# Strassen products for w of layer 1 and for both wide products of layer 2, and layer 1's weights normalised ahead of its product

## The chip, the cores and the metric

One core of one Trainium2 chip. The metric is the device time of one execution in microseconds (us). Times are medians of the fast executions on one chip; one execution of all fell in the slow state, and it is named and left out. "TensorE records" are the records of matmuls in the trace: each f32 matmul leaves two (before, the 16 matmuls of layer 2's product for v leave 32, from 1280.02 us on).

## The reference, cut to what matters

128 graphs of 64 nodes with 512 features each, and an adjacency (64 x 64) for each graph, pass through four graph layers. Each layer works on h = relu(layer norm of x) and is added to x.

```python
h = maximum(_layernorm(x), 0); x = x + _L0(h, adj, ...)   # layer 0: 512 -> 1024 -> 512
# layer 1
y = x @ w;  s = y @ a                                     # x here is h
A = exp(leaky(tanh((s_i + s_j) / 8) * 8)) * A_shape
A = A / sum(A, -1) * sum(A_shape, -1)
out = A @ x @ w                                           # w is 512 x 512
# layer 2
query, keyt, value = x @ Wq.T + bq, x @ Wk.T + bk, x @ Wv.T + bv
weight = adj * exp(query @ keyt.T)
out = (weight / sum(weight, 2)) @ value
# layer 3: three products of 512 x 512 with Wk[0..2] on x, T x, T T x
```

The inputs make b2, the bias of layer 0's second product, zero.

## The kernel before

Everything is f32. Sixteen groups of 512 rows (four tiles of 128) go through layers 0 and 1 first ("first half"), x is written to memory, and then all groups go through layers 2 and 3 ("second half"). The "change of half", some 1200 to 1400 us into the run, is where the last groups of the first half and the first groups of the second are worked on together.

Layers 0 and 3 already use Strassen's method in Winograd's form: a product of 2 x 2 blocks takes seven block products instead of eight, with sums of blocks before (in the code `comb`) and additions of the products after it (`U`, `emit`). Layer 1's product with w and layer 2's products for q (Wq and Wk folded into one matrix, `wg`) and v are plain:

```python
    def layer1(g):
        ...                                   # scores: dots with w a, tanh, leaky, exp
        for s in HALVES:
            dve(0.42, lambda s=s: nc.vector.tensor_mul(PT.t[s, :, s], z.t[s], ad.t[s, 1]), ...)
        dve(0.42, lambda: nc.vector.tensor_reduce(rows.t, ad.t[:, 0], AX.X, ALU.add), [ad], [rows])
        pd = col_sums(PT, PTk)                # four one-column matmuls
        ...                                   # sc = rows / pd, 128 x 4
        for t in range(T):
            ph = left_mul_T(hs[t], lambda t=t: PT.t[:, t, :], PTk, "mT")
            proj(lambda c, ph=ph: ph.t[:, c, :], lambda c: w_sb[:, c, :], p, ...)   # 4 matmuls of 512 columns
            dve(0.75, ... xx = p * sc + xx)   # the scale is put on the output
    def layer2(g):
        ...
        for o in range(KD):                   # q: 4 x 4 matmuls of 512 columns
            proj(lambda c, oc=oc: wg_sb[:, c, oc], lambda c: hT.t[:, c, :], pq, ...)
            ...
        for t in range(T):                    # v: 4 x 4 matmuls of 512 columns
            proj(lambda c, t=t: hT.t[:, c, tok(t)], lambda c: wv_sb[:, c, :], p, ...)
```

The program orders its own instructions while it is built. Every operation states its engine, a cost in us and a precedence number (`G.prio`, lower goes first). A list scheduler repeatedly takes, for each engine, the operation that can start earliest, and uses the precedence only among those that could start at the same time:

```python
                    if t0 is None or (t, o.prio, o.seq) < (t0, pick.prio, pick.seq):
                        t0, pick = t, o
    ...
    STRETCH, PERIOD1, PERIOD2 = 2.5, 80.0, 60.0
    for g in range(NG):
        ...
        G.prio = g * PERIOD1
        layer0(g); layer1(g)
    load_w("wg", ...); load_w("wv", ...)      # over w1's place
    olds2 = [keys of w2 and its sums, keys of w]
    ... loads of Wk3 (layer 3's weights) over olds2 ...
    W3 = combine("w3", ...)                   # four block sums of the weights on VectorE
    for g in range(NG):
        G.prio = NG * PERIOD1 + g * PERIOD2
        layer2(g); layer3(g)
```

Each engine gets its queue in that order.

Of the kernel before, what the change touches and what calls it, by code (L numbers as in the profile page):

```python
# [13 lines left out]
P = 128  # L14
C = 64
# [139 lines left out]
def tile_adj_preln_d4(  # L155
# [17 lines left out]
        "x": ([P, D], 8), "adj": ([P, 2, T, C], 3), "h": ([P, D], 5), "o": ([P, D], 2),  # L173
        "u5": ([P, 3, D], 1), "u2": ([P, 3, D // 2], 2), 
# [3 lines left out]
    }  # L178
    TWO = [
        (("tmp", [P, D], 4), ("s3", [P, 3, 6, P], 1)),  # L180
        (("z", [P, DH], 2), ("hT", [P, KD, T * P], 1)),
        (("rT", [P, KH, P], 3), ("a3", [P, 3 * KD, P], 2)),
        (("s2", [P, 3, 4, P], 1), ("vu", [P, D], 3)),
        (("y", [P, D], 2), ("qT", [P, T * P], 2)),
        (("mT", [P, KD, P], 3), ("a3", [P, 3 * KD, P], 1)),
        (("s1", [P, 3, 2, P], 2), ("tt", [P, T, 2, P], 1)),
# [4 lines left out]
    for old, new in TWO:  # L191
        size = lambda shape: shape[1] * (shape[2] if len(shape) > 2 else 1) * (shape[3] if len(shape) > 3 else 1)
        both = work.tile([P, max(size(old[1]) * old[2], size(new[1]) * new[2])], F32, name=f"{old[0]}_{new[0]}")
        for tag, shape, n in (old, new):
            for i in range(n):
                v = both[:, i * size(shape):(i + 1) * size(shape)]
                if len(shape) == 3:
                    v = v.rearrange("p (a b) -> p a b", a=shape[1])
                elif len(shape) == 4:
                    v = v.rearrange("p (a b c) -> p a b c", a=shape[1], b=shape[2])  # L200
                slots.setdefault(tag, []).append(v)
        after.setdefault(new[0], []).append(old[0])
# [12 lines left out]
    w_sb = view(WB, 7168, KD, D)  # L215
    wg_sb = view(WA, 0, KD, D)
    wv_sb = view(WA, 2048, KD, D)
# [9 lines left out]
    def c_v(n, from_psum=False):  # L227
        return n / 960 + (0.22 if from_psum else 0.16)
# [32 lines left out]
    sel = const.tile([2, 2, P], F32, name="sel")  # L261
    for i in range(2):
        nc.vector.tensor_copy(sel[:, i, :], ident[0:2, i:i + 1].to_broadcast([2, P]))
# [4 lines left out]
    def load_w(name, sb, src, olds=()):  # L268
        k, n = src.shape[0] // P, src.shape[1]
        v = src.rearrange("(c p) o -> p c o", p=P)  # L270
        for c in range(0, k, 2):
            dma(2 * n / 2, lambda c=c: nc.sync.dma_start(sb[:, c:c + 2, :], v[:, c:c + 2, :]), [], [(name, c // 2), *olds])
# [4 lines left out]
    def load_row(name, src):  # L277
        sb = const.tile([P, src.shape[0]], F32, name=name)
        dma(P * src.shape[0] * 4 / 1024, lambda: nc.sync.dma_start(sb, src.partition_broadcast(P)), [], [name])
        return sb  # L280
# [37 lines left out]
    b1_b = load_row("b1_b", b1)  # L318
# [4 lines left out]
    b2_b = load_row("b2_b", b2)  # L323
# [5 lines left out]
    wa_b = const.tile([P, D], F32, name="wa_b")  # L329
# [3 lines left out]
    bw2_b = const.tile([P, D], F32, name="bw2_b")  # L333
# [26 lines left out]

    def setup_l0():


        p, row = Buf("ps"), Buf("o")
# [10 lines left out]
        pe(c_mm(512, 1), lambda: nc.tensor.matmul(pm.t, sel[:, 0, :], row.t[0:2, :], start=True, stop=True), [row], [pm])  # L375
        pe(c_mm(512, 1), lambda: nc.tensor.matmul(pb.t, sel[:, 1, :], row.t[0:2, :], start=True, stop=True), [row], [pb])
        act(0.6, lambda: nc.scalar.copy(bw2_b, pb.t), [pb], ["bw2"])
# [5 lines left out]
    def spread(col, dst, r, key):  # L383
# [5 lines left out]
        act(0.6, lambda: nc.scalar.copy(dst, p.t), [p], [key])  # L389

    def setup_l1():
        wa, a_b = Buf("col"), temp(a.partition_broadcast(P))
        for c in range(KD):
            dot(lambda c=c: w_sb[:, c, :], lambda: a_b.t, lambda c=c: wa.t[:, c:c + 1], [("w", c // 2), a_b], [(wa, c)])
        spread(lambda: wa.t, wa_b, [(wa, c) for c in range(KD)], "wa")
# [22 lines left out]
    def setup_l3():  # L418
# [3 lines left out]
        for s in range(2):  # L422
# [5 lines left out]
            spread(lambda cc=cc: cc.t, c3_b[:, s, :], [(cc, c) for c in range(KD)], ("c3", s))  # L428
# [44 lines left out]

    def strassen(A, keys, B, kc, n, stag, emit):

# [11 lines left out]
        def prod(p, lhs, kl, b, first):  # L487
            rhs, kb = B[b]

            def mm():  # L490
                for c in range(kc):
                    nc.tensor.matmul(p.t[:, :n], lhs()[:, c, :], rhs(c), start=first and c == 0, stop=c == kc - 1,  # L492
                                     skip_group_check=True)
            pe(c_mm(n, kc), mm, [*kl, *kb] if first else [*kl, *kb, p], [p])
            step(c_mm(n, kc))

        p1, p2, p3, p4 = (Buf("ps") for _ in range(4))
        c1, u2, u3 = ((U, i) for i in range(3))
        prod(p1, a[0, 0], keys[0, 0], "11", True)
# [4 lines left out]
        act(n / 1200 + 0.17, lambda: nc.scalar.copy(U.t[:, 0], p1.t[:, :n]), [p1], [c1])  # L504
        prod(p2, s2, [(S, 1)], "T2", True)
        dve(c_v(n, True), lambda: nc.vector.tensor_add(U.t[:, 1], p2.t[:, :n], U.t[:, 0]), [p2, c1], [u2])  # L506
# [386 lines left out]
```

## Time and profile before

| | before |
|---|---|
| time, median of 3 | 2655.7 us (2651.23 to 2656.02) |
| profiled execution, span | 2648.8 us, clock 1.0 |
| TensorE busy, records | 2628.4 us, 10970 |
| VectorE busy | 1503.4 us |
| GpSimd busy | 520.6 us |

The kernel's fast executions spread from 2650.6 to 2656.2 us, on every chip about as wide (28 executions on four chips). The ratios below carry that as part of their interval.

The prediction shows the page and TensorE's waits. The busy times of the engines in a stretch stand in one line: TensorE, TensorE's weight loads, VectorE, ScalarE, GpSimd with the number of instructions behind each, then TensorE's clock, the DMA share and GB/s.

```profile
1200.00:1500.00 300.00, 297.18 (x1213) 200.00 (x1212) 154.70 (x376) 83.81 (x141) 37.26 (x55) 1.00 0.13 46
```

TensorE's order in time is shown by start, duration, source line, output and inputs, shape, number of records, and in brackets an idle time with what ended it.

```profile
1302.35 1.88 PE L636 MATMUL ps<-y_qT,bd 128*128 128x512 f32 x4
1304.07 3.60 PE L471 MATMUL ps<-wa_mem,z_hT 128*128 128x512 f32 x8
1307.50 3.94 PE L696 MATMUL ps<-y_qT,z_hT 128*128 128x128 f32 x32
1311.28 0.60 PE L541 MATMUL ps<-dg,ones_bd 128*128 128x256 f32 x2
1313.17 1.05 PE L562 MATMUL ps<-ones,bd 128*128 128x1 f32 x8 [1.29 <-DVE bd L703]
```

L636 is layer 0's last product, L541 the score product of layer 1's last group. Between the two lies a serial chain: x, its statistics, h, the dots with w a (the vector w times a, which the scores need). During its 7 to 9 us TensorE works at layer 2's first group, a plain product for q (L471, 3.4 us) and its scores (L696, 3.8 us), and L541 comes without a wait. Only layer 2's own column sums (L562) wait 1.3 us. So plain products of layer 2 hide layer 1's last chain.

### The profile page before, as it was taken

What the parts mean: (1) busy time and instruction counts of PE and PEld (TensorE: products, weight loads), DVE (VectorE), ACT (ScalarE), POOL (GpSimd) and SP (SyncE); (2) the same over time, 40 slices, a digit from 0 to 9 for tenths busy, and PEclk for the clock granted to TensorE, in tenths of its full rate; (3) what the DMA queues carried; (4) which work ended last, traced back from release to release, by engine and by line L of the source; (5) the groups of instructions that cost most, each with busy time, mean ns of one, the idle gap of its engine ahead of it and who ended that gap; (6) DMA issues with size and microseconds to landing.
All of it is one profiled execution on the core that took longest, in us unless ns stands there. A gap on an engine that the chain in (4) does not pass through costs nothing.

```text
span 2648.8 us, 28910 instructions
## 1 busy us (share of the span) xinstructions
PE 2628.4 (99%) x10970; PEld 1826.4 (69%) x10970; DVE 1503.4 (57%) x3618; ACT 787.4 (30%) x1338; POOL 520.6 (20%) x651
## 2 busy tenths in 40 slices
PE   8999999999999999999999999999999999999999
PEld 5666666666666666666567767777677766777677
DVE  8777676667666666766445443454435444354434
ACT  3343333334233333333222222222222222222221
POOL 4222223323222332222101111110111111111101
PEclk9999999999999999999999999999999999999999
DMA  4021100011100001111021000100011001100000
GB/s 159 33 92 36 36 24 17 32 37 36 36 29 22 27 32 37 36 36 44 28 84 36 29 28 33 36 20 28 25 36 36 20 21 32 36 32 16 21 24 25
DMA packets 53196, 95.99 MB, mean 36 GB/s; under 512 B 7744, under 2 KB 7744, under 8 KB 53056
## 3 DMA queue, kind: packets, MB, share of 16 engines
q1 hardware_dynamic: 53056, 94.14, 10.5%
q8 instruction: 86, 1.41, 0.2%
q14 instruction: 54, 0.44, 0.0%
HBM read 59.52 MB, written 34.60 MB: 36 GB/s over the span
## 4 chain that ended last, share of the span: by engine, by line
PE 99%; DVE 1%; ACT 0%; issue 0%; DMA 0%; DVEq 0%; ACTq 0%
PE ps L492 51%; PE ps L471 25%; PE ps L460 4%; PE ps L770 4%; PE ps L696 2%; PE ps L716 2%; PE ps L624 2%; PE ps L636 2%; PE ps L681 1%; PE ps L761 1%; PE ps L562 1%; PE ps L751 1%; PE ps L584 1%; PE ps L404 1%; PE ps L541 1%; PE ps L371 0%
## 5 line engine op out<-in xcount | busy, mean ns | idle before, releaser
L443 POOL TENSOR_TENSOR rs<-ve,mhalf 128x1 f32<-128x1 f32 x320 | 213.9, 671 | 1408.5 <-DVE ve L442 1376.3
L492 PE MATMUL ps<-wb_mem,rT_a 128*128 128x256 f32 x2056 | 472.7, 379 | 1.0 <-ACT u L504 1.0
L492 PEld LDWEIGHTS ps<-wb_mem,rT_a 128*128 128x128 f32 x2056 | 386.0, 190 | 61.9 <-issue 6.2
L451 ACT ACTIVATE h<-x,nm,rs 128x512 f32<-128x512 f32 x256 | 205.4, 811 | 356.5 <-DVE nm L450 353.7
L492 PE MATMUL ps<-wb_mem,tmp_s 128*128 128x256 f32 x1152 | 263.8, 379 | 0.0
L492 PEld LDWEIGHTS ps<-wb_mem,tmp_s 128*128 128x128 f32 x1152 | 215.6, 190 | 34.0 <-issue 4.1
L440 DVE BATCH_NORM_STATS2 st<-x 128x6 f32<-128x512 f32 x256 | 175.5, 686 | 110.5 <-DMA x<-xm 109.8
L492 PE MATMUL ps<-wa_mem,mT_a 128*128 128x512 f32 x512 | 237.9, 593 | 0.0
L471 PE MATMUL ps<-wa_mem,z_hT 128*128 128x512 f32 x512 | 228.2, 592 | 0.2 <-ACT z_hT L683 0.2
L471 PE MATMUL ps<-wb_mem,mT_a 128*128 128x512 f32 x512 | 227.4, 592 | 0.0
L471 PE MATMUL ps<-z_hT,wa_mem 128*128 128x512 f32 x512 | 227.3, 592 | 0.0
L492 PE MATMUL ps<-wb_mem,s_vu 128*128 128x256 f32 x768 | 180.1, 380 | 0.0
L492 PE MATMUL ps<-wa_mem,s_tt 128*128 128x512 f32 x384 | 177.7, 593 | 0.4 <-DVE s_tt L485 0.4
L471 PEld LDWEIGHTS ps<-wb_mem,mT_a 128*128 128x128 f32 x512 | 96.1, 190 | 114.8 <-issue 114.3
L471 PEld LDWEIGHTS ps<-z_hT,wa_mem 128*128 128x128 f32 x512 | 95.0, 190 | 101.7 <-issue 100.9
L471 PEld LDWEIGHTS ps<-wa_mem,z_hT 128*128 128x128 f32 x512 | 94.8, 190 | 100.4 <-issue 99.0
L492 PEld LDWEIGHTS ps<-wa_mem,mT_a 128*128 128x128 f32 x512 | 93.7, 190 | 100.0 <-issue 100.0
L492 PEld LDWEIGHTS ps<-wb_mem,s_vu 128*128 128x128 f32 x768 | 143.5, 190 | 21.4 <-issue 2.4
L460 PEld LDWEIGHTS ps<-bd,h 128*128 128x128 f32 x1024 | 129.3, 194 | 40.0 <-issue 34.7
L462 ACT COPY mT_a<-ps 128x512 f32<-128x512 f32 x128 | 74.6, 583 | 246.8 <-PE ps L460 206.6
L532 POOL TENSOR_TENSOR u<-u,bk_b 128x256 f32<-128x256 f32 x96 | 71.2, 757 | 365.0 <-DVE u L506 189.9
L460 PE MATMUL ps<-bd,h 128*128 128x128 f32 x1024 | 133.0, 278 | 4.3 <-ACT h L451 4.1
(163 smaller groups left out, 3525.1 us busy)
## 6 DMA issues: line engine op xcount, KB each, us to landing
x<-in_x_dram SPq DMA_DIRECT2D x64, 256.0 KB, 2.6
xm<-x SPq DMA_DIRECT2D x64, 256.0 KB, 2.0
x<-xm SPq DMA_DIRECT2D x64, 256.0 KB, 2.6
out_dram<-x SPq DMA_DIRECT2D x64, 256.0 KB, 2.0
adj<-in_adj_dram SPq DMA_DIRECT2D x32, 256.0 KB, 2.5
wb_mem<-in_Wk_dram SPq DMA_DIRECT2D x6, 512.0 KB, 7.2
wa_mem<-in_W1T_dram SPq DMA_DIRECT2D x2, 1024.0 KB, 8.1
wb_mem<-in_W2T_dram SPq DMA_DIRECT2D x4, 512.0 KB, 6.2
```

The costliest lines, as they stand in the source:

```text
L440: dve(0.69, lambda i=i: nc.vector.bn_stats(st.t[:, i, :], src(i)), [r[i]], [(st, i)])
L443: pool(0.57, lambda: nc.gpsimd.tensor_tensor(rs.t, ve.t, mhalf, ALU.pow), [ve], [rs])
L451: act(0.82, lambda: nc.scalar.activation(h.t, xx.t, AF.Relu, bias=nm.t, scale=rs.t), [xx, nm, rs], [h])
L460: nc.tensor.matmul(quad(p)[:, c, :], h.t[:, c * P:(c + 1) * P], rhs(), start=True, stop=True)
L462: act(0.59, lambda: nc.scalar.copy(m.t, quad(p)), [p], [m])
L471: nc.tensor.matmul(p.t, lhsT(c), rhs(c), start=first and c == 0, stop=last and c == k - 1)
L492: nc.tensor.matmul(p.t[:, :n], lhs()[:, c, :], rhs(c), start=first and c == 0, stop=c == kc - 1, skip_group_check=True)
L532: pool(0.75, lambda: nc.gpsimd.tensor_add(U.t[:, iv], U.t[:, iu], row[:, cols]), [u, krow], [v])
L624: nc.tensor.transpose(quad(pt)[:, c, :], z.t[:, j * D + c * P:j * D + (c + 1) * P], ident)
L636: pe(c_mm(512, 1), lambda y=y, pf=pf, t=t: nc.tensor.matmul(pf.t, M.t[:, t, :], y.t, start=True, stop=True), [(y, 0), (y, 1), *Mr], [pf])
L696: nc.tensor.matmul(quad(pl)[:, t, :], hT.t[:, o, tok(t)], qT.t[:, tok(t)], start=(o == 0 and t == 0), stop=(o == KD - 1), skip_group_check ...
L770: nc.tensor.matmul(pq.t[:, c * 2 * P:(c + 1) * 2 * P], h.t[:, cc * P:(cc + 1) * P], tt.t[:, t].rearrange("p j k -> p (j k)"), start=True, ...
```

## The change

The intent: 7/8 of the matmul work in three more products. TensorE is the bound (99% busy before), VectorE (57%) and GpSimd (20%) have time left for the extra sums. In layer 1 the scale of the output goes into the weights first, so that the additions after the Strassen products need no scale. In layer 2 the four block sums of h are shared by q and v (`sh`). The diff, cut to its core:

```diff
-        PT, rows, sc = Buf("bd"), Buf("col"), Buf("col")
+        PT, pd, rn = Buf("bd"), Buf("ps"), Buf("ee")
+        dve(0.42, lambda: nc.vector.tensor_mul(z.t, z.t, ad.t[:, 1]), [z, ad], [z])
+        def sums():
+            for i, m in enumerate((lambda: z.t, lambda: ad.t[:, 1])):
+                nc.tensor.matmul(pd.t[:, i * T * C:(i + 1) * T * C], ones_bd, m()..., start=True, stop=True)
+        pe(c_mm(256, 2), sums, [z, ad], [pd])
+        dve(2.0, lambda: nc.vector.reciprocal(rn.t, half(0)), [pd], [rn])
+        dve(0.42, lambda: nc.vector.tensor_mul(rn.t, rn.t, half(1)), [pd, rn], [rn])
         for s in HALVES:
-            dve(0.42, lambda s=s: nc.vector.tensor_mul(PT.t[s, :, s], z.t[s], ad.t[s, 1]), [z, ad], ...)
+            dve(0.42, lambda s=s: nc.vector.tensor_mul(PT.t[s, :, s], z.t[s], rn.t[s]), [z, rn], ...)
-        for t in range(T): ... proj(..., w_sb, ...)
+        for t0 in (0, 2):
+            ph = [left_mul_T(hs[t], ...) for t in (t0, t0 + 1)]
+            strassen(lambda i, j, ph=ph: ph[i].t[:, 2 * j:2 * j + 2, :], ..., W, 2, D // 2, "s1", emit_w)
@@ layer2
+        X = Buf("sh")                          # four sums of blocks of h, for q and v
+        for q, (a, ka, b, kb, op) in enumerate(...):
+            dve(c_v(D), lambda ...: nc.vector.tensor_tensor(X.t[:, q], a(), b(), op), ...)
-        for o in range(KD): ... proj(lambda c, oc=oc: wg_sb[:, c, oc], ...)
+        seven({n: prod(WG[n], hs[n], True) for n in range(1, 8)}, Buf("u5"), D, emit_q)
-        for t in range(T): ... proj(..., lambda c: wv_sb[:, c, :], ...)
+        seven({n: prod(WV[n], hv[n], False) for n in range(1, 8)}, Buf("u5"), D, emit_v)
@@ memory: which buffers of the second half (right) lie over which of the first (left)
-        (("s2", [P, 3, 4, P], 1), ("vu", [P, D], 3)),
-        (("s1", [P, 3, 2, P], 2), ("tt", [P, T, 2, P], 1)),
+        ([("s2", [P, 3, 4, P], 1), ("s1", [P, 3, 2, P], 2)], [("vu", [P, 2, D], 2), ("tt", [P, T, 2, P], 1)]),
+        ([("row", [P, D], 5)], [("sh", [P, 4, 2, 2 * P], 1)]),
-    wa_b = const.tile([P, D], F32, name="wa_b")
+    wa_b = Buf("row")                          # the row w a, which layer 1's dots read
@@ order and loads
-    STRETCH, PERIOD1, PERIOD2 = 2.5, 80.0, 60.0
+    STRETCH, PERIOD1, PERIOD2 = 2.5, 80.0, 65.0
+    W = combine("w", w_sb, w_x, 2, D // 2, "DVE")
+    WG, WV = combine_hT("wg", wg_sb, wg_x, True), combine_hT("wv", wv_sb, wv_x, False)
-    olds2 = [keys of w2 and its sums, keys of w]
+    olds2 = [keys of w2 and its sums, keys of w and its sums]
```

## The prediction

> **What bounds the kernel now.** I read the page first (busy shares, then the 40 slices), then the waits of TensorE, the stretches in which each engine was busy, and the order of TensorE's instructions in time.
>
> ```profile
> span 2648.8 us, 28910 instructions
> PE 2628.4 (99%) x10970; PEld 1826.4 (69%) x10970; DVE 1503.4 (57%) x3618; ACT 787.4 (30%) x1338; POOL 520.6 (20%) x651
> PEclk9999999999999999999999999999999999999999
> PE ps L584 <- DVE mB L579: 5.9, 1, 5.9
> PE ps L460 <- ACT h L451: 4.1, 2, 3.7
> PE ps L770 <- ACT s_tt L753: 1.4, 2, 0.7
> 300.00:1100.00 800.00, 800.00 (x3279) 530.62 (x3278) 545.86 (x1325) 284.82 (x488) 223.50 (x263) 1.00 0.09 32
> 1480.00:2480.00 1000.00, 1000.00 (x4267) 729.03 (x4266) 452.63 (x1114) 245.96 (x414) 121.74 (x168) 1.00 0.09 29
> ```
>
> TensorE is busy 99% of the span at an ungated clock (the windows give 1.00). Its longest wait is 5.9 us, once, at the very start; the nine waits in the whole list sum to about 16 us. In the two long windows (layers 0 and 1; then layers 2 and 3) it never stops, while VectorE has 32% and 55% left. So the time is the sum of TensorE's instructions plus a small fixed rest. What must be found is what one instruction costs in the stream. The duration in the group rows (379 ns for 256 columns, 592 for 512) is not that: consecutive matmuls overlap. I take start-to-start distances:
>
> ```profile
> 602.70 1.89 PE L492 MATMUL ps<-wb_mem,rT_a 128*128 128x256 f32 x8
> 604.42 1.89 PE L492 MATMUL ps<-wb_mem,s_vu 128*128 128x256 f32 x8
> 606.15 1.02 PE L636 MATMUL ps<-y_qT,bd 128*128 128x512 f32 x2
> 607.01 0.59 PE L541 MATMUL ps<-dg,ones_bd 128*128 128x256 f32 x2
> ...
> 685.25 0.59 PE L541 MATMUL ps<-dg,ones_bd 128*128 128x256 f32 x2
> ...
> 1280.02 13.90 PE L471 MATMUL ps<-z_hT,wa_mem 128*128 128x512 f32 x32
> 1293.76 3.60 PE L471 MATMUL ps<-wa_mem,z_hT 128*128 128x512 f32 x8
> ```
>
> Each f32 matmul leaves two records. 32 records of 512 columns take 1293.76-1280.02 = 13.74 us, 0.4294 each; 16 of 256 columns take 606.15-602.70 = 3.45 us, 0.2156 each. So a matmul costs 0.859 us at 512 columns and 0.431 at 256: cost goes with columns, halving the columns costs nothing extra, and a Strassen product of narrower matmuls is not punished. The same line of one group recurs after 685.25-607.01 = 78.24 us: one group's period in the first half. In the second half the row-sum line recurs after 83.8 us (1730.93 to 1814.73). Sixteen groups each: 16 x (78.24+83.8) = 2592.6; setup matmuls, start, change of half and tail make the rest of the 2648.8.
>
> [...] of the four block sums of 128x256 in layer 0, one kind takes 635 ns and another 415 (one line, L485)[...].
> [...] the reciprocal[...]. No run here yet shows a wide one; the narrow one (128x4) takes 178 ns against 162 for a product of that size.
>
> **The change, part by part.**
> *Layer 1, product with w.* Per group before: 4 tiles x 4 matmuls of 512 columns = 16 x 0.859 = 13.74 us. After: 2 pairs of tiles x 7 products x 2 matmuls of 256 columns = 28 x 0.431 = 12.07. Saved 1.67. The column sums (4 one-column matmuls, 8 records in 0.80 us) become two 256-column matmuls, 0.86: net saved 1.6 us.
> *Layer 2, q and v products.* Before: 2 x 16 x 0.859 = 27.49 us. After: 2 x 7 products x 4 matmuls of 256 columns = 56 x 0.431 = 24.14. Saved 3.3 us. The order of the changed program confirms the counts: 512-column matmuls fall from 1373 to 605, those of 256 rise from 2528 to 3904; other sizes change only by those 64 one-column ones.
> *Sum on TensorE.* -768 x 0.859 + 1376 x 0.431 - 12.8 = -659.7+593.1-12.8 = -79 us[...]. I use 78: new periods 76.7 and 80.5 us.
> *VectorE, layer 1, per group.* Added: 8 block sums of 128x256 at about 0.50 (mean of the four L485 kinds), 4 additions to U and 8 final ones at 0.42, one product of 128x256 at 0.42, a second at 0.42, and a reciprocal of 128x256.[...] Removed: 4 x 0.75, a row reduction 0.41, two small ones 0.34. Net about +8.4 us.
> *VectorE, layer 2, per group.* Added: 4 shared sums and 4+7 additions of 128x512 at 0.69 = 10.35; removed 4 x 0.69: +7.6. Total 16 x 16 = 256 us: busy goes from 1503 to about 1760 us, 68%. In the first half it is 545.9/800 x 78.24 = 53.4 per period, and 62 of 76.7 after (80%); in the second 37.9, and 45.5 of 80.5 (57%). Beside TensorE, therefore, not ahead of it.
> *GpSimd.* +6 additions of 128x256 (0.75) in layer 1, +6 of 128x512 (1.3) in layer 2: +12 us per group, 520 to about 715 us, 28%. ScalarE: about the same.
> *Setup.* Four more weight sums for w (1.2 us each, as the other 128x1024 ones), ten of 128x512 for layer 2: some 13 us of VectorE, at the start and at the change of half, with other work open. Both loads of layer 2 weights are there before and after.
>
> **What could eat the 78 us.** The sum holds only if TensorE still never waits. I walked the narrowest places of the new order by hand. In layer 2 the last transposes of h are followed by one layer 3 product (12 records, 2.59 us), then by the product that needs two shared sums. Copy out of PSUM begins about 0.2 after the transposes and takes 0.59, two sums take 1.35, hand-overs 0.2: 2.3 us of 2.59. For the first score matmuls of a combined q: after the seventh product U is added (0.2+0.65), GpSimd adds the bias (1.3), VectorE adds q (0.69), with 0.2 of hand-overs 3.0 us; two products lie between, 3.45 us. Both fit, with 0.3 to 0.5 us to spare.[...]
>
> **Rivals.**
> *A: Narrow chains and the GpSimd lock bring waits in every group.* For: slack of a third of a us, two engines more loaded[...], one slot each for U and for the shared sums. Against: the scheduling gave TensorE an unbroken 1800 us in the two windows, and costs stated in the code equal the trace (0.42, 0.69, 1.3). At 1 us per group in both halves 16-32 us return: 2594 to 2610.
> *B: VectorE becomes the bound in the first half.* For: 80% there, in order[...]. Against: 20% is left, and work of neighbouring groups is mixed. A third of the gain lost would mean about 2604.
> *C: The change of half gets longer,* because block sums now stand between loads and first products. For: about 5 us of small waits lie there today (1265, 1311, 1347 us). Against: raw blocks come first in the new order, combined ones some 12 us of TensorE work later. Worth 0 to 6 us: 2578 to 2584.
> *D: No gain, as narrower matmuls cost more each.* The spacings above refute it; it would give about 2655.
>
> **Range and chances.** 2655.7-78.0 = 2577.7. I add 3 us for small waits (C and a little of A): 2581. If start and change of half go better: 2568; if A takes a us per group all over: 2605. Two per cent lies at 2602.6, which needs 25 us of new waits. Chances: 0.89 faster, 0.10 within, 0.01 slower.
>
> **What would show it right or wrong.** Right: TensorE has 12058 records and 98 to 99% busy, clock 1.00; 256-column records still 0.216 apart in the new products; period about 76.7 and 80.5 us; VectorE near 1760 us, GpSimd near 715; waits below 40 us in all. Step by step: [...]additions 0.42 and 0.69. Wrong: a wait in the list of TensorE's waits that comes 16 times (behind the shared sums, behind q, behind the normalised weights) would mean A or B; a gap near the middle, C; a spacing of more than 0.22 us, D; a granted clock under 1.00, something I have not considered.

Cut from it is what it said of the hardware that no trace here shows, and the terms that rested on that. VectorE's sum for layer 1 came to +8.4 us a group, and from it the 62 us per period (80%), the 256 us and the 1760 us; its term for the wide reciprocal is cut, and the terms left give +6.1. TensorE's sum came to 78 us: the terms left, rounded, give 79, and the two finer costs that gave 78.0 are cut. The mean spacings in the trace before (0.8587 and 0.4318 us a matmul, from neighbouring records of one line and shape within 10% of the median, 300 to 1100 and 1480 to 2480 us) give 78.1. "The GpSimd lock" is a name for what the trace before shows of the kind of sums that take 635 ns on average: 13 of the 32 take 0.95 us, and each ends 0.28 us after an addition of 128x256 on GpSimd (L532, 0.78 us) beside it; the other 19 take 0.42.

## The result

| | before | after |
|---|---|---|
| time, median | 2653.47 us (4 runs) | 2608.65 us (4 runs, 2606.12 to 2608.72) |
| profiled span | 2648.8 us | 2606.9 us |
| TensorE records | 10970 | 12058 |
| VectorE, GpSimd busy | 1503.4, 520.6 us | 1771.4, 710.4 us |

The result is right, and the ratio is 0.9829 (0.9812 to 0.9846). A ratio is the mean time of one kernel's fast runs over that of the other's fast runs of the same rounds, so it is not quite the ratio of the medians. The change gains 1.7%, less than the 2.8% predicted, and 2608.65 us is 3.7 above the 2605 that the prediction took as its worst case. A gain under 2% counts as "same" here, to which the prediction gave a chance of 0.10.

The page after, in the lines that answer to those of before:

```profile
span 2606.9 us, 32072 instructions
PE 2562.2 (98%) x12058; PEld 2047.3 (79%) x12058; DVE 1771.4 (68%) x4064; ACT 783.4 (30%) x1370; POOL 710.4 (27%) x843
PEclk9999999999999999999989999999999999999999
```

One slice of the clock, just past the middle, is no longer 9. TensorE's waits after (who waited <- for what: us in all, times, longest):

```profile
PE ps L871 <- ACT h L493: 9.9, 1, 9.9
PE ps L635 <- DVE mB L630: 6.1, 1, 6.1
PE ps L555 <- DVE s_s_vu_tt L547: 5.5, 7, 1.0
PE ps L592 <- DVE dg L590: 4.3, 1, 4.3
PE ps L502 <- DVE bd L715: 2.4, 1, 2.4
```

The 6.1 us are the start, as before. New are one of 9.9 us, one of 4.3, one of 2.4, one of about 1 us that comes seven times, and a few of 1.4 us and less that are not shown. The windows after:

```profile
300.00:1100.00 800.00, 796.14 (x3543) 584.27 (x3542) 642.38 (x1506) 298.77 (x517) 277.14 (x329) 1.00 0.10 32
1480.00:2480.00 1000.00, 1000.00 (x5048) 870.53 (x5047) 566.22 (x1313) 248.13 (x443) 211.52 (x249) 1.00 0.09 30
1200.00:1500.00 300.00, 278.38 (x1354) 232.65 (x1353) 191.81 (x433) 81.57 (x144) 64.88 (x81) 0.96 0.14 46
```

The second half is perfect: 1000 us without a pause. The first half loses 4 of 800 us. At the change of half TensorE is busy 278 of 300 us at a mean clock of 0.96; before it was 297 at 1.00.

Busy time hides part of a loss, so I also counted gaps: for each pair of neighbouring TensorE records in a trace, the distance of their starts less what that kind takes in the undisturbed stream (0.429 us a record at 512 columns, 0.216 at 256, 0.109 at 128), summed by stretch. "Undisturbed" is the sum of those spacings.

| us | undisturbed sum | gaps 0 to 200 | 200 to 1200 | 1200 to 1500 | 1500 to end | gaps, total |
|---|---|---|---|---|---|---|
| before | 2616.1 | 10.4 | 2.0 | 5.4 | 4.5 | 22.3 |
| after | 2538.0 | 14.6 | 8.1 | 32.3 | 3.0 | 58.0 |
| difference | -78.0 | +4.2 | +6.1 | +26.9 | -1.5 | +35.7 |

The 78.0 us of the prediction are there to a tenth of a us. They are taken back, 35.7 us of them, nearly all at the change of half. 78.0 less 35.7 is 42.3; the spans of the two profiled executions differ by 41.9.

### What happens at the change of half

TensorE's order, after:

```profile
1274.04 1.88 PE L687 MATMUL ps<-y_qT,bd 128*128 128x512 f32 x4
...
1281.99 1.22 PE L592 MATMUL ps<-dg,ones_bd 128*128 128x256 f32 x2 [4.35 <-DVE dg L590]
1283.00 7.17 PE L773 MATMUL ps<-row_sh,wa_mem 128*128 128x256 f32 x24
1290.01 1.89 PE L773 MATMUL ps<-wa_mem,row_sh 128*128 128x256 f32 x8
...
1340.21 1.04 PE L871 MATMUL ps<-ident,h 128*128 128x128 f32 x8
1351.12 1.12 PE L871 MATMUL ps<-ident,h 128*128 128x128 f32 x4 [9.87 <-ACT h L493]
```

L687 is the last product of layer 0, L592 the score product of layer 1's last group, with the same serial chain between them as before. This time TensorE has nothing to do in it: the products of layer 2 that need no block sum (L773 with `z_hT`) had gone in earlier, among the products of layer 0, and the next ones (L773 with `row_sh`) need the shared block sums. VectorE in these us, after:

```profile
1280.77 0.69 DVE L351 SCALAR_TENSOR_TENSOR o<-h,row_sh 128x512 f32<-128x512 f32 x1
...
1281.51 0.42 DVE L590 TENSOR_TENSOR dg<-ident,col 128x256 f32<-128x256 f32 x1
1281.85 0.69 DVE L758 TENSOR_TENSOR row_sh<-z_hT 128x512 f32<-128x512 f32 x1
```

L351 is layer 1's last dot: it reads the row w a, which lives in the memory `row_sh`. L758 is layer 2's first shared sum: it writes into `row_sh`, since the change laid the buffer of these sums over the rows. It cannot start before the last dot has read that row. That is a wait which the diff makes and which no list of TensorE's waits names.

TensorE idles. Then a second price is seen: the 24 records of L773 from 1283.00 take 7.01 us up to the next group, where 24 at 0.216 would take 5.2. Record by record, some nine of them are 0.427 us apart: a stretch at half speed, called a cold start below (a name only). From 1280 to 1300 us the granted clock is 0.83, and it is 0.50 in an earlier short stretch too:

```profile
1280.00:1300.00 20.00, 18.01 (x84) 15.84 (x85) 10.66 (x19) 2.36 (x6) 4.81 (x5) 0.83 0.00 1
1252.60:1256.00 3.40, 3.40 (x13) 3.01 (x13) 1.97 (x4) 2.90 (x5) 0.01 (x1) 0.50 0.54 177
```

In the first, nine records of 0.427 us are 3.8 us at half speed. The length of the wait does not sort these stretches: the one from 1252.6 us is slow after waits of only 0.4 and 1.4 us (in the 3.5 us before it TensorE was busy 1.7), while the clock stays at 1.00 after one of 2.4 us at 1309.0. So these traces give no threshold, and what brings the clock down and back was not shown. By the count of the table above, the wait at 1278 cost 4.5 us and its cold start another 2.4.

The longer wait, at 1341, has another cause. The chain of waits that ended last, in order of time (start, duration, what), after:

```profile
1342.04 1.68 DVE wb_mem L363
...
1347.32 1.76 DVE wb_mem L366
1349.08 0.62 DVE st L482
...
1351.12 1.12 PE ps L871 x4
```

L363 to L366 are the four block sums of layer 3's weights, 7 us on VectorE. They wait for the load of the weights, and that load waits for layer 1's last use of w (before the change too; now for the sums of w as well). In VectorE's queue they stand ahead of the statistics (L482) of a tile of x, whose h TensorE needs for layer 3's first group. Before, the same four sums ran from 1355.5 us on, behind layer 3's first score product (L541 at 1337.1), and nobody waited. In the changed kernel the wait cost 10.0 us by the same count, and the slow stretch after it 4.1, of which 0.5 are a wait for a shared sum. The two places together are 21.0 of the 32.3 us; the rest lies at 1249 to 1259 (4.4), at 1307 (2.7) and at 1324 to 1332 (2.7). How much of the 14.1 is due to the sums, run e4 tells.

### The small wait in the first half

It comes about once in two groups, for example ending at 337.2, 491.5 and 646.1 us, so some 154.4 us for two groups, 77.2 for one (predicted 76.7). It ends with a block sum of layer 0 (L547), which stands in VectorE's queue behind two long ones. VectorE, then GpSimd in the same time, after (L651, of 1.43 us, from 640.18 on, runs beside the first sum, L652 beside the second):

```profile
640.40 1.76 DVE L547 TENSOR_TENSOR rT_a<-rT_a 128x512 f32<-128x512 f32 x1
642.08 1.75 DVE L547 TENSOR_TENSOR s_s_vu_tt<-rT_a,s_s_vu_tt 128x512 f32<-128x512 f32 x1
```

```profile
641.69 1.60 POOL L652 TENSOR_TENSOR x<-x,row_sh 128x512 f32<-128x512 f32 x1
```

Two sums that take 0.69 us when alone take 1.76 and 1.75 while GpSimd adds. Each ends 0.55 us after the addition beside it has ended (640.18 + 1.43 and 641.69 + 1.60), as if it did most of its work only then; all 24 long sums of this shape in the trace do so. That looks like the lock of rival A.

### The profile page after: what moved, and what is told of

It is laid out like the page before. It is cut to its first block, busy times and chain, and to the rows that moved or that the text cites. A ratio compares the mean times of both kernels' runs of the same rounds, so it can differ in the third digit from the quotient of the medians.

```text
span 2606.9 us, 32072 instructions
## 1 busy us (share of the span) xinstructions
PE 2562.2 (98%) x12058; PEld 2047.3 (79%) x12058; DVE 1771.4 (68%) x4064; ACT 783.4 (30%) x1370; POOL 710.4 (27%) x843
## 4 chain that ended last, share of the span: by engine, by line
PE 95%; DVE 4%; issue 0%; ACT 0%; POOL 0%; DVEq 0%; ACTq 0%; POOLq 0%
PE ps L555 58%; PE ps L773 15%; PE ps L880 4%; PE ps L502 4%; PE ps L826 2%; PE ps L796 2%; PE ps L687 2%; PE ps L675 2%; PE ps L745 1%; PE ps L871 1%; DVE st L482 1%; DVE s_s_vu_tt L547 1%; PE ps L861 1%; PE ps L709 1%; PE ps L446 1%; PE ps L592 1%
## 5 line engine op out<-in xcount | busy, mean ns | idle before, releaser
L485 POOL TENSOR_TENSOR rs<-ve,mhalf 128x1 f32<-128x1 f32 x320 | 208.1, 653 | 937.4 <-DVE ve L484 896.7
L555 PE MATMUL ps<-wb_mem,s_s_vu_tt 128*128 128x256 f32 x1152 | 276.4, 379 | 0.1
L555 PEld LDWEIGHTS ps<-wb_mem,s_s_vu_tt 128*128 128x128 f32 x1152 | 215.6, 190 | 40.7 <-issue 7.5
L555 PE MATMUL ps<-wb_mem,mT_a 128*128 128x256 f32 x1016 | 242.9, 379 | 0.0
L482 DVE BATCH_NORM_STATS2 st<-x 128x6 f32<-128x512 f32 x256 | 174.4, 686 | 62.7 <-DMA x<-xm 61.2
L555 PEld LDWEIGHTS ps<-wb_mem,mT_a 128*128 128x128 f32 x1016 | 190.0, 190 | 34.0 <-issue 7.7
L555 PE MATMUL ps<-wa_mem,s_s_vu_tt 128*128 128x512 f32 x384 | 178.3, 594 | 5.5 <-DVE s_s_vu_tt L547 5.5
L527 DVE TENSOR_TENSOR u<-ps,u 128x512 f32<-128x512 f32 (+1 forms) x160 | 84.7, 529 | 115.6 <-PE ps L555 90.5
L502 PEld LDWEIGHTS ps<-bd,h 128*128 128x128 f32 x1024 | 130.2, 195 | 32.7 <-issue 18.7
L585 DVE TENSOR_TENSOR o<-ps,u 128x256 f32<-128x256 f32 x96 | 40.7, 424 | 153.5 <-PE ps L555 149.7
L726 POOL TENSOR_TENSOR x<-x,u 128x256 f32<-128x256 f32 x96 | 70.0, 742 | 259.2 <-DVE u L525 197.4
L555 PEld LDWEIGHTS ps<-wa_mem,s_s_vu_tt 128*128 128x128 f32 x384 | 71.9, 190 | 86.1 <-issue 68.6
```

The costliest lines, as they stand in the source:

```text
L482: dve(0.69, lambda i=i: nc.vector.bn_stats(st.t[:, i, :], src(i)), [r[i]], [(st, i)])
L485: pool(0.57, lambda: nc.gpsimd.tensor_tensor(rs.t, ve.t, mhalf, ALU.pow), [ve], [rs])
L502: nc.tensor.matmul(quad(p)[:, c, :], h.t[:, c * P:(c + 1) * P], rhs(), start=True, stop=True)
L527: dve(c_v(n), lambda: nc.vector.tensor_add(at(2)(), p4.t[:, :n], at(1)()), [p4, (U, 1)], [(U, 2)])
L555: nc.tensor.matmul(p.t[:, :n], lhs()[:, c, :], rhs(c), start=first and c == 0, stop=c == kc - 1, skip_group_check=True)
L726: pool(0.75, lambda: nc.gpsimd.tensor_add(xx.t[:, cols], xx.t[:, cols], U.t[:, iu]), [xx, u], [xx])
```

## The experiments

Theories, before the first run. (1) The load: that of layer 3's weights waits for layer 1's last product with w, which now ends later against the second half's work, and so holds up the W3 sums and what stands behind them. (2) The order: at the change of half products of layer 2 are used up too early, so that none lie beside the last and first serial chains. (3) The added sums of the weights themselves (layers 2 and 3) fill VectorE at the change of half. (4) The lock, for the small waits. A fifth came after the twelfth run: (5) the reuse of memory seen above is what leaves TensorE without work beside layer 1's last chain. The gaps of each run, from its trace:

| us | 0 to 200 | 200 to 1200 | 1200 to 1500 | gaps, total | time, median | ratio to before (95%) |
|---|---|---|---|---|---|---|
| after | 14.6 | 8.1 | 32.3 | 58.0 | 2608.65 | 0.9829 (0.9812 to 0.9846) |
| e1 layer 1 alone | - | - | - | - | 2644.66 (3 runs) | 0.9967 (0.995 to 0.9984) |
| e2 layer 2 alone | 12.3 | 2.0 | 12.1 | 29.4 | 2605.03 | 0.9815 (0.98 to 0.983) |
| e3 Wk earlier | 13.6 | 8.0 | 26.3 | 51.0 | 2602.81 | 0.9807 (0.9793 to 0.9822) |
| e4 no weight sums | 14.3 | 8.0 | 28.6 | 53.9 | 2603.67 | 0.9811 (0.9795 to 0.9827) |
| e5 second half later | 13.4 | 8.1 | 14.5 | 39.0 | 2589.76 | 0.9757 (0.9742 to 0.9771) |
| e6 e3 and e5 | 14.2 | 8.1 | 9.3 | 34.6 | 2584.76 | 0.9736 (0.9722 to 0.9751) |
| e7 before, later | 12.3 | 2.0 | 3.6 | 22.4 | 2650.84 | 0.9986 (0.9971 to 1.0001) |
| e8 e6 without layer 1 | 11.9 | 2.0 | 6.0 | 23.0 | 2599.03 | 0.9792 (0.9776 to 0.9808) |
| e9 e6, tiny additions | 12.1 | 1.0 | 9.3 | 25.4 | 2577.72 | 0.9716 (0.97 to 0.9732) |
| e10 e6, tuned order | 12.2 | 8.3 | 10.4 | 34.5 | 2583.52 | 0.9737 (0.9722 to 0.9751) |
| e11 e6, scale last | 17.7 | 17.1 | 9.7 | 47.6 | 2594.71 | 0.9778 (0.9764 to 0.9793) |
| e12 e1, later | 13.3 | 8.1 | 8.0 | 32.6 | 2636.18 | 0.9935 (0.992 to 0.995) |
| e13 e6, w a apart | 14.7 | 8.1 | 9.7 | 35.5 | 2584.40 | 0.9739 (0.9724 to 0.9753) |
| e14 after, 20 later | 14.3 | 8.1 | 28.3 | 53.7 | 2602.93 | 0.9807 (0.9791 to 0.9824) |
| e15 e14, w a apart | 12.6 | 8.1 | 19.9 | 43.6 | 2595.82 | 0.9781 (0.9766 to 0.9796) |

e1 to e4 ran together on one chip, so did e5 to e8, e9 to e12, and e13 to e15; the kernel before had medians of 2654.15, 2655.68, 2653.26 and 2653.32 beside them. The profiled execution of e1 (2928.6 us, clock 0.886) is left out of the median; its three other runs were fast, 2644.5 to 2646.6. "After" ran on its own, so compare across chips by the ratios.

### e1 and e2: each layer's part alone

```diff
 e1: layer 2, its weights and buffers as before; layer 1 changed
 e2: layer 1 and its weights as before; layer 2 changed
```

> The changed kernel with layer 2 as before (four whole products of 512 columns for q and v, no sums of their weights); layer 1 as changed. TensorE's work falls by 26.7 us against before (16 x (1.65 + the shorter column sums)). Theory D, the drain: layer 1's new form lengthens what stands between the last group's layer 0 and its last output (a wide reciprocal ahead of the products, pairs of tiles), so that TensorE finds nothing ready at the change of half; then most of the gain is lost already here: the gaps at 1200 to 1450 us are 15 us or more above before (which has 5), and the time is 2637 to 2648. Theory S, the one-off sums of layer 2 weights on VectorE stand in the way: they are not in this kernel, so the gaps stay near 5 us and the time falls by the whole 26 us, to about 2628.

> The changed kernel with layer 1 as before (whole products with w, normalised at the end); layer 2 as changed. TensorE's work falls by 52.7 us against before. Theory D: the change of half is longer by 3 to 8 us only, the time is 2604 to 2610, so about the same as the whole change (2608.65) with 25 us more of TensorE's work. Theory S: nearly all of the 27 us of new gaps is here, and the time is about 2625.

Of the 78.0 us less TensorE work, layer 1's part is 25.3 and layer 2's 52.6 (sums of the spacings). Layer 1's part alone gained 9.5 us (2654.15 to 2644.66, fast runs), layer 2's alone 49.1. The whole change is no faster than layer 2's part alone (0.9829 and 0.9815, intervals that overlap). So layer 1's part earns next to nothing where it stands, and layer 2's nearly all. That does not say yet that layer 1's arithmetic is to blame: with layer 1's part, the gaps at the change of half grow from 12.1 to 32.3 us. The wait for L590 is not among what layer 1's part adds: e2 has it too, with 5.2 us.

### e3: the load of layer 3's weights doesn't wait for w

The raw loads go over w2's place, free earlier; only the first sum, which writes where w's was, waits for w.

```diff
-    olds2 = [keys of w2 and its sums, keys of w and its sums]
+    olds2 = [keys of w2 and its sums]
+    olds3 = [keys of w and its sums]
-    W3 = combine("w3", w3_sb, w3_x, 6, D // 2, "DVE")
+    W3 = combine("w3", w3_sb, w3_x, 6, D // 2, "DVE", olds3)
```

> The changed kernel, but the raw blocks of layer 3's weights are loaded as soon as layer 0's second weights are done with (their places do not overlap w), and only the sums of them wait for w. Same instructions, other order. Theory W: the load that waits for layer 1's last use of w holds up layer 3 of the first group, and with it all that follows; then the gap of 10 us near 1341 us shrinks to 2 or less and the time falls by 10 to 15 us, to about 2595. If the load is hidden anyway, the time stays within 5 us of 2608.

Some 6 us come back, less than half of the gap at 1341, and neither the 10 to 15 us nor the "within 5" of the expectation. The wait of 9.9 us is gone, but another has come (TensorE's waits, e3):

```profile
PE ps L773 <- DVE s_s_vu_tt L816: 8.5, 1, 8.5
```

The sums of layer 3's weights now run from 1323.3 us on and stand in VectorE's queue ahead of an addition of v (L816) instead of ahead of the statistics of h. Moving the block of 7 us moves the wait. Theory 1 alone is refuted as the cause, though the wait it names is real.

### e4: without the sums of the weights

The four sums for layer 3 and the ten for layer 2 are left out; the result is wrong.

```diff
-        G.op(eng, cost, lambda: sub(x_[:, 1], ...), ...)   # and the three after it, for w3
-            v(lambda: add(x_[:, 0], ...), ...)             # and the others, for wg and wv
```

> The changed kernel without the one-off sums on VectorE of layer 3's and layer 2's weights (14 operations, about 14 us of VectorE); the products read old contents, so the result is wrong on purpose. Theory S: their 14 us stand on the path, and the time falls by 10 us or more, to 2598 or less. Theory D: they fill time in which VectorE's chain waits for something else, and the time falls by 5 us at most, to 2603 to 2609.

Even with no sum there, the gaps at the change of half are 28.6 us, and the time falls by 0.2%. Theory 3 falls: the sums of the weights are not the main cause. Two of TensorE's waits in e4, whose line numbers are 10 lower (L861 is L871 above, L735 is L745):

```profile
PE ps L735 <- ACT h L483: 3.8, 2, 3.4
PE ps L861 <- ACT h L483: 1.8, 1, 1.8
```

In place of the wait of 9.9 us stand three, of 1.8 us for an h of layer 3's first group, of 1.0 for its scores (L582) and of 3.4 for an h of layer 2's next group, and from 1340 to 1358 us the gaps are 10.7 us where the changed kernel has 14.1. So some 3.5 us of that loss are the sums; the larger part is there without them: serial chains of x, its statistics and h, with no work of TensorE beside them.

### e5, e6 and e7: the second half later in precedence

One line: all operations of layers 2 and 3 get a precedence number 80 higher, so the first half's are preferred for longer. e6 has e3's edit as well. e7 is the control: the same line in the kernel before.

```diff
-        G.prio = NG * PERIOD1 + g * PERIOD2
+        G.prio = (NG + 1) * PERIOD1 + g * PERIOD2
         layer2(g)
```

> The changed kernel with one number changed: all operations of layers 2 and 3 stand 80 us (one group's period) lower in the order of precedence, so that they go only where the first half leaves TensorE free, instead of being mixed into the last group's layer 0. Same instructions, same places in memory. Theory D, the drain: in the changed kernel the products of layer 2's first group are spent beside layer 0, where TensorE has enough to do, and are then missing beside the chain of layer 1's last group; then this order gives back half or more of the gaps at 1200 to 1450 us (32 us now) and the time falls by 12 to 20 us, to 2589 to 2597. Theory N, the work itself (more of VectorE for each group) makes the chains too long for any order: the gaps move but do not shrink, and the time stays within 4 us of 2608.

> e3 and e5 together. If they fill different gaps, as I think (e3 the wait for layer 3's weights, e5 the missing products), the gaps at 1200 to 1450 us fall to about 10 us and the time to 2578 to 2584, which is what the prediction gave for a change of half no longer than before. If they fill the same gap, the time is that of e5.

> The kernel before with the same shift of precedence as e5: a control. It has only 5 us of gaps there, so at most 4 us can come back: 2649 to 2655. If it falls by 10 us or more, e5 would be a gain of its own that has nothing to do with the change.

One line brings the ratio from 0.9829 to 0.9757, and with e3's edit to 0.9736: the gaps at the change of half go from 32.3 to 14.5 and to 9.3 us. In the kernel before the same line leaves the gaps at 22.4 (22.3), though those at the change of half fall there too, by 1.8 us; its runs, all near 2651, lie at the lower end of that kernel's spread, and the interval of the ratio includes 1, so no gain is shown. So the order suited the kernel before and no longer suits the changed one. The change of half in e6:

```profile
1200.00:1500.00 300.00, 293.20 (x1470) 247.88 (x1470) 199.65 (x452) 85.75 (x153) 67.44 (x85) 1.00 0.15 49
```

and of TensorE's waits of e6:

```profile
PE ps L592 <- DVE dg L590: 2.6, 1, 2.6
```

The same chain of layer 1's last group costs 2.6 us instead of 4.3, and the clock stays at 1.00, so nothing is added for a cold start. The waits of 9.9 and 2.4 us are gone. Theory 2 holds: with another order most of the loss is gone. Theory 1's wait adds to it: in e5 the four sums of layer 3's weights (1320.8 to 1328.0 us) still stand ahead of a tile's statistics, TensorE waits 5.6 us for h (L745) and starts cold, 8.3 of the 14.5 us. With the early load they run from 1303.1 us on and cost one wait of 2.1 us (L796, for q). e6 is 5 us faster than e5, 0.8 us short of what was expected.

### e8 and e12: layer 1's part with the order mended

e8 is e6 with layer 1 as before; e12 is e1 with the later second half.

> e2 (layer 2 changed, layer 1 as before) with the shift of e5 and the early load of e3. Beside e6 it tells what layer 1's part is worth once the order is mended. Its work on TensorE is 25.3 us more than e6's. Theory D: layer 1's part lost its gain to the order only; then this one is 12 to 20 us slower than e6: 2594 to 2602. Theory N: layer 1's part is worth nothing by its own longer chain; then both are within 5 us.

> The kernel of e1 (layer 1 changed alone; 8.5 us gained of 25.3 us less TensorE work, 2645.6) with the second half 80 later in precedence. If the rest of e1's loss was, as in the whole change, the order at the change of half, about 8 us come back: 2636 to 2641, near the 14.3 us that layer 1 was worth between e8 and e6. If it was the first half (GpSimd and VectorE), it stays at 2644 to 2647.

From e8 to e6, layer 1's part is worth 14.3 us (2599.03 to 2584.76); alone, from 9.5 us (e1) it goes to 17.1 (2653.26 to 2636.18; 14.7 against e7, which has the later second half too). The rest of its 25.3 us is seen in the gaps: e6 has 11.6 us more of them than e8, of which 6.1 lie between 200 and 1200 us. The small waits for L547 (L548 in e12) are in e6 and e12, eight times, and not in e8 or e2 at all: they come with layer 1's part.

### e9: GpSimd's two additions made tiny

On e6; every engine keeps its order, instruction by instruction. Its output is wrong, which doesn't matter for the time.

```diff
-                pool(1.3, lambda xx=xx, h=h: nc.gpsimd.tensor_add(xx.t, xx.t, h.t), ...)
-                pool(1.3, lambda xx=xx: nc.gpsimd.tensor_add(xx.t, xx.t, b2_b.t), ...)
+                pool(1.3, lambda xx=xx, h=h: nc.gpsimd.tensor_add(xx.t[:, :1], xx.t[:, :1], h.t[:, :1]), ...)
+                pool(1.3, lambda xx=xx: nc.gpsimd.tensor_add(xx.t[:, :1], xx.t[:, :1], b2_b.t[:, :1]), ...)
```

> On the kernel of e6 (2584.8 us), GpSimd's two additions to x in layer 0 (x + h, then + b2; 128x512, 1.4 and 1.6 us each, 128 in all) are narrowed to one column. Instruction order is the same on every engine; the result is wrong on purpose. Lock theory ([...]the eight waits of TensorE for the block sums of layer 0, about 0.9 to 1.2 us each): the waits go, layer 0's 128x512 block sums come back near 0.69 us, TensorE's gaps from 200 to 1200 us fall from 8.1 to about 2, time 2577 to 2580. Rival (VectorE is just too late in its own queue there, lock or none): the block sums may get shorter elsewhere but the eight waits stay, time 2583 to 2586.

The lock theory, that these additions stretch VectorE's sums from 0.69 to 1.75 us and so make the waits, holds: the time falls by 7 us to 2577.7, and the gaps from 200 to 1200 us from 8.1 to 1.0. One kind of layer 0's sums (shortest, median and longest ns), first e6, then e9:

```profile
L547 DVE TENSOR_TENSOR s_s_vu_tt<-rT_a,s_s_vu_tt x32: 677/685/1761, 57.6 to 1256.9; 128x512 f32<-128x512 f32 x32
```

```profile
L547 DVE TENSOR_TENSOR s_s_vu_tt<-rT_a,s_s_vu_tt x32: 682/684/693, 56.9 to 1247.6; 128x512 f32<-128x512 f32 x32
```

The longest goes from 1761 to 693 ns; nothing else was touched on VectorE. Its busy time falls by 42 us in all (1769.8 to 1727.4): what this pair of additions cost VectorE. Of the 128 sums of 128x512, 23 take over 1 us in e6 and none in e9. What it is in the additions that holds the sums up was not isolated.

### e10: a tuned order

On e3, other precedence numbers: stretch 1.89, layer 1 14 earlier, layers 2 and 3 58.2 later, layer 3 another 58.6.

```diff
-    STRETCH, PERIOD1, PERIOD2 = 2.5, 80.0, 65.0
+    STRETCH, PERIOD1, PERIOD2 = 1.89, 80, 65
         layer0(g)
+        G.prio += -14.0
         layer1(g)
-        G.prio = NG * PERIOD1 + g * PERIOD2
+        G.prio = NG * PERIOD1 + g * PERIOD2 + 58.2
         layer2(g)
+        G.prio += 58.6
         layer3(g)
```

> The kernel of e6 with other precedence numbers only: a stretch of 1.89 in place of 2.5, layer 1 14 earlier, second half 58.2 later in place of 80, layer 3 another 58.6 later. If what is left at the change of half in e6 (9 us of gaps beyond TensorE's own work from 1200 to 1500 us) is a matter of order, it comes to about 2579 or less; if e6 is as good as order gets and the rest is the chains of dependences, 2584 to 2590. The eight waits of the first half should stay, as nothing is done to the additions on GpSimd, unless the order moves them apart.

No gain over e6 (0.9737 and 0.9736). The gaps only move: TensorE is busy 799.9 us from 300 to 1100 (e6: 796.1), and between 1100 and 1200 us there are now 4.3 us of gaps. These other numbers are no better than e6's; whether others are was not tried.

### e11: the scale on the outputs again

On e6: the weights stay unnormalised, and the scale is put on each output block, as before the change.

```diff
-        dve(2.0, lambda: nc.vector.reciprocal(rn.t, half(0)), [pd], [rn])
-        ...
+        pd = col_sums(PT, PTk)
+        ...                                     # sc = rows / pd, 128 x 4
-                pool(0.75, lambda: nc.gpsimd.tensor_add(xx.t[:, cols], xx.t[:, cols], U.t[:, iu]), [xx, u], [xx])
-                dve(c_v(D // 2), lambda: nc.vector.tensor_add(xx.t[:, cols], p.t[:, :D // 2], xx.t[:, cols]), [p, xx], [xx])
+                scaled(lambda: xx.t[:, cols], xx, lambda: sc.t[...], [sc], lambda: xx.t[:, cols], [xx], p, u, v, D // 2)
```

> The kernel of e6 with the weights of layer 1 unnormalised again and the scale put on the outputs of the product with w, as before the change did, now on each block of the Strassen product. This takes away the 128x256 reciprocal (1.75 us), one product (0.42) and two 256-column matmuls (0.86 us) per group, and brings back four one-column ones (0.80), a row reduction and two small ones (0.75), and puts six additions of 128x256 per group on VectorE that GpSimd did (6 x 0.42). VectorE has about 1 us more per group, TensorE 1 us less in all. Theory (normalising first is a matter of which engine works, and TensorE has no wait on it in the steady state): within 5 us of e6, 2580 to 2590. Rival (the six more on VectorE, 80% busy in the first half already, tip it over): more waits in the first half, 2592 or more. Another (the reciprocal of 1.75 us in the serial chain costs something at the change of half): 2578 to 2583.

10 us slower than e6: the time lies where the second expectation (tipped over) put it, and the first failed. TensorE's longest entry of e11, and the kind of sums shown for e6 and e9:

```profile
PE ps L555 <- DVE s_s_vu_tt L547: 12.3, 11, 2.0
L547 DVE TENSOR_TENSOR s_s_vu_tt<-rT_a,s_s_vu_tt x32: 678/1216/1761, 58.7 to 1273.9; 128x512 f32<-128x512 f32 x32
```

VectorE's busy time from 300 to 1100 us is 653.5 us against e6's 642.4, 82% against 80%, and the gaps from 200 to 1200 us double, 8.1 to 17.1. But that VectorE was tipped over is not shown. The median sum takes 1216 ns instead of 685: of the 128 sums of 128x512, 41 take over 1 us here, 23 in e6; that GpSimd's additions hold up these too is the author's reading, not tried on e11. From 300 to 1100 us these sums take 85.1 us in all, in e6 70.9, and VectorE's busy time grows by only 11.1. So longer sums account for its growth; whether more work on VectorE alone would cost anything, no run tells (e11 with e9's tiny additions would). Normalising first is worth some 10 us in this order.

### e13, e14 and e15: the row w a in memory of its own

The rows keep four slots, w a gets one of its own, so the shared sums no longer wait for layer 1's last dot. With the precedence of the change as it is this edit leaves no order that can run (an early operation of layer 2 takes buffers that layer 1 needs), so it was tried with the second half 20 later: e14 is the change with 20 alone, e15 has the edit too. e13 is the edit on e6.

```diff
 e14, e15
-        G.prio = NG * PERIOD1 + g * PERIOD2
+        G.prio = NG * PERIOD1 + g * PERIOD2 + 20.0
         layer2(g)
 e13, e15
-        ([("row", [P, D], 5)], [("sh", [P, 4, 2, 2 * P], 1)]),
+        ([("row", [P, D], 4)], [("sh", [P, 4, 2, 2 * P], 1)]),
-    wa_b = Buf("row")
+    wa_b = Buf("wa")
```

> The kernel of e6 with the row w a (read by the last dots of layer 1) in memory of its own, so that the buffer of layer 2's shared block sums, which lies over the rows, no longer waits for layer 1's last group. Reuse theory (this sharing is why TensorE has nothing to do beside layer 1's last chain): the shared sums of layer 2's first group run before the last dg, the wait for dg (2.6 us) goes or shrinks below 1 us, 2580 to 2583. Order theory alone (e6's order is what counts, and with it the sharing costs little): within 1.5 us of e6 (2584.8, ratio 0.9736).

> The changed kernel with the second half 20 later in precedence (e5: 80), nothing else: base for the next run. By the order theory it lies between the changed kernel (0.9829) and e5 (0.9757): ratio 0.977 to 0.982. Gaps at the change of half between 15 and 30 us.

> The run before with the row w a in memory of its own (without any lateness that edit leaves no order at all, as an early operation of layer 2 then takes buffers that layer 1 needs; hence 20). Reuse theory: with an order that starts layer 2 early, the sharing is what leaves TensorE idle beside layer 1's last chain (4.4 us and some 2 at half speed in the changed kernel), so 5 to 10 us are gained over the run before and the wait for dg goes. Order theory alone: within 3 us of the run before, and the wait for dg stays.

VectorE's first shared sum (L758) and layer 1's last score column (L590), e14, then e15:

```profile
1277.87 0.42 DVE L590 TENSOR_TENSOR dg<-ident,col 128x256 f32<-128x256 f32 x1
1278.21 0.68 DVE L758 TENSOR_TENSOR row_sh<-z_hT 128x512 f32<-128x512 f32 x1
```

```profile
1267.79 0.69 DVE L758 TENSOR_TENSOR row_sh<-z_hT 128x512 f32<-128x512 f32 x1 [0.63 <-ACT z_hT L747]
...
1284.10 0.43 DVE L590 TENSOR_TENSOR dg<-ident,col 128x256 f32<-128x256 f32 x1
```

In e15 the sums come 16 us ahead of L590, products of layer 2 fill TensorE from 1269.6 us on, and the wait of 4.3 us for L590, which e14 has as the changed kernel does, is gone with its cold start. Gaps at the change of half fall by 8.4 us, the time by 7.1, as theory 5 said. On e6 the same edit takes the wait of 2.6 us away, but one of 2.8 us for layer 2's own weights of attention comes instead, and the time stays (0.9739 and 0.9736): there the order had already mended what the reuse cost, and the first expectation of e13 failed. The wait of 9.9 us for h is in e15 as before; it belongs to layer 3's first chain, with the four sums in front of its statistics.

## Why the prediction was wrong

**The sum was right.** 12058 records, 78.0 us less in undisturbed spacing, VectorE 1771.4 us (predicted 1760, or 1773 with the 13 us of setup that it named and did not add), GpSimd 710.4 (715), 0.216 us for a record of 256 columns in the new products. Rival D is refuted, as the prediction said. The spacings it shows double to 0.8588 and 0.4312 and give 79 us; the 78.0 came out.

**The second half was right.** Its row-sum line recurs after 80.5 us (1743.55, 1824.06, 1904.57), the very period predicted, and 1000 us pass without a pause. The narrow places that the prediction walked by hand, two shared sums and the q chain, hold.

**The step that failed is rival C's size.** The prediction gave the change of half "Worth 0 to 6 us" and added 3 us for C and a little of A. It measured 26.9 us. Two of its signs of being wrong appeared: a gap near the middle, and a clock under 1.00, which it had not considered. Its reason against C, that raw blocks come first and combined ones some 12 us of TensorE work later, looked only at the sums that layer 2's first products need, and not at the serial chains of the neighbours. What failed was the hiding of these chains, and it failed in two places. Beside layer 1's last chain TensorE had no work, as the shared sums were laid over a row that this chain reads: 4.5 us and 2.4 of cold start; without the reuse 8.4 us of gaps go (e15). And layer 3's first chain had none either, with the sums of layer 3's weights ahead of its statistics in VectorE's queue: 10.0 us and 4.1 after it, of which 10.7 stay without any sums (e4). Freeing the load of these weights earlier alone leaves a wait of 8.5 us elsewhere (e3); a later second half leaves waits of 2.6 and 5.6 us (e5), both edits together 2.6 and 2.1 and no cold start at the change of half (e6). Together these two places are 21.0 of the 32.3 us of gaps there; the rest are waits of 2.4 us and less and one more cold start.

The evidence could have been had. The prediction quotes layer 2's plain products from 1280 to 1297 us, and reads them only for their spacing; the next two blocks, from 1304 us, are what hid layer 1's chain. And the diff shows `row` under `sh`. The prediction checked each new operation's cost and none of the new reuses.

**Rival A happened in a small form.** Waits of about 1 us, not one a group in both halves (16 to 32 us) but one in two groups in the first half: +6.1 us. GpSimd's two additions cause them: with these made tiny, the gaps from 200 to 1200 us are 1.0 us instead of 8.1 (e9).

**Rival B is not shown.** VectorE is at 80% in the first half, as it said, but with GpSimd's two additions made tiny TensorE never pauses from 300 to 1100 us, and VectorE is still at 78% (e9). The loss in e11 comes with more long sums (41 of over 1 us, in e6 23).

**Other terms.** The wide reciprocal (L712, 128x256) took 1.75 us, less than the term that is cut, and TensorE is still busy 796.1 of the 800 us from 300 to 1100; the start took 4.2 us more. What these consist of was not isolated: e7, whose start is that of the kernel before, already has 12.3 us of gaps there instead of 10.4, so differences of 2 us, as between e6 and e9, say nothing.

Of the miss, 2608.65 less 2581, 27.7 us: gaps grew by 35.7 where 3 were allowed, 32.7 too many. By luck 5 of them are hidden: the quoted 2655.7 lay at the upper end of the kernel before's spread, while its profile was taken at the lower end (2650.59).

What stays open: why, with the same load and the same wait for w, the sums of layer 3's weights come ahead of layer 3's first statistics only when layer 1's part is in (gaps of 12.1 in e2, 32.3 with it), which I can only put down to the order; how much of that is PERIOD2, which the change also moved from 60 to 65 (no run has the old number); why the small waits come once in two groups and not in each; and how much of the 9.3 us at the change of half in e6 an order not tried could hide.

## What to carry to other kernels

When a change shortens the work of the engine that is the bound, walk the order at every boundary between stages, not only the steady state: ask which work lies beside each serial chain there, and whether the change takes it away, moves it or gives it something to wait for, a reused buffer included. If the kernel orders itself, its precedence numbers belong to the kernel they were tuned on; one number (e5) brought back 19 of the 35.7 us lost here, and the best version found, e6, is 2.6% faster than before where the change as given is 1.7%. Before you put a loss down to an engine's load, compare the shortest and the longest duration of one and the same instruction: here (0.69 and 1.76 us) the difference was GpSimd's additions beside it (e9). An addition that another engine does can still cost the first one time: these two cost VectorE 42 us.

## What these traces show of the hardware

- The granted clock was 0.50 for 3.4 us after waits of 0.4 and 1.4 us, and 1.00 after one of 2.4, and of 2.6 in e6. After an idle time of 4.4 us about nine records of 256 columns were 0.427 us apart. Each f32 matmul leaves two records, 0.429 us apart at 512 columns and 0.216 at 256.
- GpSimd's two additions to x in layer 0 cost VectorE 42 us of its 1770 in e6. The 24 long sums of 128x512 in the changed kernel each end 0.55 us after the GpSimd addition beside them has ended.
- The reciprocal of 128x256 on VectorE took 1.75 us.
- At 128x512 a GpSimd addition with the bias of a row took 1.27 us (L814), one with a broadcast column 1.05 (L787).
